# One core, four graph layers in fp32: the second group of tokens shares resident tiles of w0, and two preparations get later keys

## The chip, the cores and the metric

The kernel runs on one core of one Trainium2 chip. The metric is the device time of one execution in microseconds (us). Three executions of the kernel before took 2164.63, 2165.2 and 2167.5 us; the median is 2165.2 us.

## What is computed

128 graphs of 64 nodes with 512 features pass through four layers; each layer adds its result to x and normalizes. Cut to what matters:

```python
# layer 0: w0 is the weight that this case is about
y = x @ w;  s = y @ a
A = exp(leaky(8 * tanh((s_i + s_j) / 8))) * adj
x = layernorm(x + (A / rowsum(A) * rowsum(adj)) @ x @ w)
# layer 1
weight = adj * exp((x @ Wq.T) @ (x @ Wk.T).T)
x = layernorm(x + weight / rowsum(weight) @ (x @ Wv.T))
# layer 2
q, k = split(X @ Wqk);  v = X @ Wv
w = mask * (q . (adj @ (k * mask))) / sqrt(512)
x = layernorm(x + softmax_over_nodes(w)[:, :, None] * v)
# layer 3: two hypergraph convolutions, 512 -> 1024 -> 512, relu and layernorm between
x = layernorm(x + conv(layernorm(relu(conv(x, W1))), W2))
```

## The kernel before, in words

The 8192 tokens are cut into 32 groups (`NG`) of 256 tokens, two tiles of 128 (`GT = 2`). `run(g)` (L1004) writes down all the work of one group as operations with an engine, a cost, what they read and write, and a key. `prepare_chunk(c)` (L699) prepares the adjacency matrices of two groups at a time: chunk 0 serves groups 0 and 1, chunk 1 groups 2 and 3.

Nothing is issued while this is written down. When everything is known, `Order.run` (L140) goes through the operations as a list scheduler: on each engine, whenever it is free in the planner's own time, the ready operation with the lowest key is taken. So each engine's instruction stream is fixed before the kernel runs, and on the chip each engine goes through its stream in order. Keys come from three places:

- For work outside the groups the key is the value of `order.key` at that point in the code: 0.0 for the first use of v1 (L561), 3.0 for m2 (L625), `BASE[GC * c] - 3.0` for the chunk c > 0 (L700), which is 1.0 for chunk 1, as `BASE[2]` is 4.
- For the work of a group, `keys_by_what_follows` (L105) sets it from how long a chain still follows in the group: the operations of group g start at `BASE[g]` (0, 2, 4, 6, 8, 12, ... for g = 0, 1, 2, ...) and spread over 16.
- Evictions of PSUM get `NOW` (100) subtracted, so that they go first. Loads of streamed weights have their user's key less 1.5.

VectorE operations that read only SBUF and all operations of GpSimd are kept from overlapping by the plan (`port`). TensorE has operations in two forms, on the whole 128 x 128 array and on its quarters or columns, and `choose` (L122) keeps to one form for a stretch. A load is planned only while its key is no more than `AHEAD` = 3.5 above the lowest step not yet started.

A product of a 256 x 512 left side with a 512 x 512 weight is done in seven block products in place of eight (`seven_products`, L848). It needs seven pieces of the weight: three of its four quarters (b11, b21, b22) and four combinations t1 to t4 of quarters, which `combine` (L490) makes with three VectorE subtractions and one of GpSimd. The left side needs four sums of its own (`side_sums`, L828; s[2] is made last, and the last of the seven products needs it).

The pieces come to the products in two ways. `prepare_first` (L544) loads the weight into the ring, makes the pieces there, and both stores them in DRAM and returns the resident pieces; group 0 uses these for w0 and v1 (`first_use`). All other groups call `streamed` (L665), which loads the stored pieces from DRAM into new ring tiles: for w0 four loads, three of 512 KB and one of 256 KB. The ring has 8 tiles of 512 KB. The resident w0 takes four (two raw, two of combinations), the resident v1 the other four. A ring tile comes free when its last planned reader is done.

`gram` (L566) multiplies two weight matrices. m2 is made from the two halves of Wqk: each half is loaded in two parts, so its matmuls come in a first half (four operations, one for each of four PSUM banks) and a second half (four more, into the same banks). Its results are copied by ScalarE, and `combine` makes its pieces. m2 is first used by group 0's layer 2.

What happens for a group in its first steps, in order: a dot product per row and two small matmuls with exponentials in between give the attention `e`; `e` is multiplied with the reciprocal of its row sums (L1036); `gathered` (L806) multiplies it on quarters of TensorE with x, ScalarE copies the two banks (gT); `left_side` makes the four sums; seven products with w0 are added to x by VectorE (`scaled_into`, L904), where the last product u goes into two blocks; `layer_norm` (two statistics, a power of -0.5 on GpSimd at L940, a VectorE product, two ScalarE passes); then the transposes (L788), the products with m1 and v1, and so on.

`prepare_chunk` makes four small VectorE operations (L706 to L709), one of GpSimd into `bh` (L711), 32 quarter matmuls (L725), their evictions, five tiny VectorE operations, and, at a key 6.0 higher, two loads of mask rows and two products for `am`, which is first read in layer 2 of the chunk's first group.

In the profile all engine instructions carry line 1178, that of the recording helper, so tile names tell them apart: `ring` is a weight piece, `k` a left side or a raw weight, `e` the attention, `m` the pieces of m1 and m2, `kept` and `bh` belong to the chunk, `w` and `v` are the stored pieces of w0 and v1 in DRAM (`v` those of v2 too).

Of the kernel before, what the change touches and what calls it, by code (L numbers as in the profile page):

```python
# [22 lines left out]
GC = CT // GT  # L23
# [5 lines left out]
BASE = [APART * g - 2 * min(g, 4) - 2 * max(g - NG + 3, 0) for g in range(NG)]  # L29
# [230 lines left out]
def kernel(  # L260
# [51 lines left out]
    order = Order({k: len(v) for k, v in kinds.items()})  # L312
# [309 lines left out]
    for h in range(2):  # L622
        load_half(wq2_raw, wqk_h[0], h)
        load_half(wk2_raw, wqk_h[1], h)
    order.key = 3.0  # L625
    m2 = gram("m2", wq2_raw, wk2_raw, KC // 2)

    order.key = 6.0
# [36 lines left out]
    def streamed(which, room=()):  # L665

        pieces = []
        chunks = KH // 2 if which == "3b" else KC // 2
        for src, n in stored[which]:
            width = PIECE // src.cells  # L670
            t_ = Buf("ring")
            order.add("SP", 500, [src[list(range(n))]], [t_, *(room if not pieces else ())],
                      lambda t_=t_, src=src, n=n, width=width: nc.sync.dma_start(
                          out=t_.t[:, : n * width], in_=src.t[:, : n * width]),
                      urgent=1.5, size=P * n * width * 4)
            for k in range(n):
                pieces.append((t_, lambda t_=t_, k=k, width=width: t_.t[:, ts(k, width)].rearrange(
                    "p (c o) -> p c o", c=chunks)))
        return pieces
# [17 lines left out]
        dma(P * T * 4, [rows], [mask_rows], lambda: mask_rows.t.rearrange("(t p) -> t p", p=P), lambda: flat(rows.t)[:T])  # L697

    def prepare_chunk(c):  # L699
        order.key = BASE[GC * c] - 3.0 if c else 0.5  # L700
        adj, turned = adjs[c], turned_adjs[c]
        m = mask_c.t[:, ts(c, CT)]
        hA, bh, am = Buf("kept"), Buf("bh", 2), Buf("kept")
        be = Buf("col")

        dve(W, [turned], [hA, turn], lambda: nc.vector.tensor_scalar(hA.t, turned.t, 0.0, None, ALU.not_equal))  # L706
        dve(W, [hA], [be], lambda: nc.vector.tensor_reduce(be.t[:, :CT], hA.t, AX.X, ALU.add))
        dve(CT, [be], [be], lambda: nc.vector.tensor_scalar(be.t[:, :CT], be.t[:, :CT], 1.0, None, ALU.max))
        dve(CT, [be], [be], lambda: nc.vector.reciprocal(be.t[:, :CT], be.t[:, :CT]))  # L709

        pool(W, [hA, be], [bh[0]], lambda: nc.gpsimd.tensor_mul(bh.t[:, :, :N], hA.t, per_tile(be.t[:, :CT])))  # L711
        act(CT, [turned], [bh[1]], lambda: nc.scalar.copy(bh.t[:, :, N : N + 1], turned.t[:, :, 0:1]))


        ps = [Buf("bank") for _ in range(2)]
        gm, sums = Buf("kept"), Buf("col")

        def quarters_of(n, at, left, right):
            for g in range(CT // 2):
                for h, (cols, _) in enumerate(halves):  # L720
                    for t, (rows, _) in enumerate(halves):
                        nc.tensor.matmul(ps[t].t[cols, at(g) : at(g) + n], left.t[rows, 2 * g + h], right(2 * g + h)[rows],
                                         start=True, stop=True)

        def emit_g():  # L725
            quarters_of(N + 2, lambda g: (N + 3) * g, hA, lambda i: bh.t[:, i])
            quarters_of(1, lambda g: (N + 3) * g + N + 2, turned, lambda i: ones)

        pe(400, [turned, hA, bh], [*ps, gm], emit_g, mode="quarters", matmuls=16)
        def per_g(t):  # L730
            return ps[t].t[:, : CT // 2 * (N + 3)].rearrange("p (g k) -> p g k", k=N + 3)

        for t in range(2):
            act(P, [ps[t]], [gm], lambda t=t: nc.scalar.copy(
                gm.t.rearrange("p (g t) i -> p t g i", t=2)[:, t], per_g(t)[:, :, :N]), NOW)
            dve(6, [ps[t]], [sums], lambda t=t: nc.vector.tensor_copy(
                sums.t[:, : 3 * CT].rearrange("p (k g t) -> p t g k", t=2, k=3)[:, t],
                per_g(t)[:, :, N:]), NOW)
        dn, n_edges, radj = (slice(CT * k, CT * (k + 1)) for k in range(3))
        g1, dc, dh = Buf("col"), Buf("col"), Buf("col")  # L740

        dve(CT, [sums], [dc], lambda: nc.vector.tensor_scalar(dc.t[:, :CT], sums.t[:, dn], TINY, None, ALU.max))
        dve(CT, [dc], [dc], lambda: nc.vector.reciprocal(dc.t[:, :CT], dc.t[:, :CT]))
        dve(CT, [sums, dc], [dc], lambda: nc.vector.scalar_tensor_tensor(
            dc.t[:, :CT], sums.t[:, dn], 0.0, dc.t[:, :CT], ALU.is_gt, ALU.mult))
        dve(CT, [dc], [dh], lambda: nc.vector.tensor_scalar(dh.t[:, :CT], dc.t[:, :CT], 0.5, None, ALU.mult))

        dve(CT, [dc, sums], [g1], lambda: nc.vector.tensor_mul(g1.t[:, :CT], dc.t[:, :CT], sums.t[:, n_edges]))

        order.key += 6.0  # L750
        mr = Buf("adj", 2)
        for h, (rows, _) in enumerate(halves):
            src = mask_rows.t.rearrange("(t h i) -> h t i", h=2, i=N)[h, ts(c, CT)]
            dma(P * CT * N * 2, [mask_rows], [mr[h]], lambda rows=rows: mr.t[rows],
                lambda src=src: bass.AP(tensor=src.tensor, offset=src.offset, ap=[[0, N], *src.ap]))
        pool(W, [adj, mask_c, turn], [am], lambda: nc.gpsimd.tensor_mul(am.t, adj.t, per_tile(m)))
        dve(W, [am, mr], [am], lambda: nc.vector.tensor_mul(am.t, am.t, mr.t))
        prepared[c] = adj, turned, gm, am, sums, g1, dc, dh
# [89 lines left out]
    def seven_products(a, s, pieces, first, more, across=False):  # L848


        going, pair = Buf("product"), [Buf("bank") for _ in range(2)]
        pieces = iter(pieces)

        def times(ps, left, start=True):
            piece, view = next(pieces)
            token = pair[ps] if isinstance(ps, int) else ps
            chunks = KH // 2 if left[2] else KC // 2
            width = PIECE // chunks if left[2] or wide else D // 2

            def emit():  # L860
                l, b, o = left[1](), view(), token.t
                if across:
                    for c in range(2):
                        for k in range(chunks):
                            nc.tensor.matmul(o[:, ts(c, P)], b[:, k, ts(c, P)], l[:, k, :],
                                             start=start and k == 0 and c == 0,
                                             stop=k == chunks - 1, skip_group_check=True)
                else:
                    for k in range(chunks):
                        nc.tensor.matmul(o[:, :width], l[:, k, :], b[:, k, :], start=start and k == 0,  # L870
                                         stop=k == chunks - 1, skip_group_check=True)

            pe(w_pe(P, 2 * chunks) if across else w_pe(width, chunks), [left[0], piece, going], [token], emit,
               matmuls=2 * chunks if across else chunks)
            return (token, going), lambda: token.t[:, :width]

        deep = a["deep"] if "deep" in a else False
        wide = a["wide"] if "wide" in a else False

        def side(v):  # L880
            return v[0], v[1], deep


        first("11", *times(0, side(a["11"])))
        first("22", *times(1, side(s[0])))
        more("11", *times(Buf("bank"), side(a["12"])))
        first("12", *times(0, side(s[1]), False))
        more("12", *times(1, side(s[3]), False))
        first("21", *times(Buf("bank"), side(a["22"])))
        u = times(0, side(s[2]), False)  # L890
        more("22", *u)
        more("21", *u)
# [11 lines left out]
    def scaled_into(at, f, own, n, base=None):  # L904


        def add(k, token, ps, base):
            dst = at[k]
            t = own.start + int(k[0]) - 1
            dve(n + 40, [*token, f, base[0]], [dst[0]], lambda: nc.vector.scalar_tensor_tensor(  # L910
                dst[1](), ps(), f.t[:, t : t + 1], base[1](), ALU.mult, ALU.add), NOW)

        return (lambda k, token, ps: add(k, token, ps, base[k] if base else at[k]),
                lambda k, token, ps: add(k, token, ps, at[k]))
# [89 lines left out]
    def run(g):  # L1004
# [20 lines left out]
        for t in range(GT):  # L1025
# [12 lines left out]
        step(1)  # L1038
        left = left_side(gathered(*of_x, lambda h, t: e.t[halves[h][0], t, :], [e]))
        step(2)  # L1040
        seven_products(*left, first_use["w0"] if g == 0 else streamed("w0"), *scaled_into(
            at_x, sums, slice(2 * CT + own.start, 2 * CT + own.stop), D // 2))
        layer_norm(xt)

# [204 lines left out]
```

## Time and profile before

| what | value |
|---|---|
| median of three executions | 2165.2 us |
| the profiled execution's own time | 2166.22 us |
| its span, first to last instruction | 2164.4 us |
| VectorE busy | 1541.9 us, 71% of the span |
| ScalarE busy | 856.9 us |
| GpSimd busy | 386.1 us |
| moved by DMA | 476.34 MB, 220 GB/s in the mean |
| granted TensorE clock, mean | 0.998 |

The profiled execution lies 1.82 us above its own span and 1.02 us above the median. After the first groups, which start closer together, results are stored at alternating distances of 65.6 and 66.0 us, one group each: 528.3, 593.8, 659.8, 725.4 us and so on up to about 1700 us. The last four groups end closer together again. A reader should look at the first 65 us by themselves: there groups 0 and 1 start, the weights arrive, and m1 and m2 are made.

### The profile page before, as it was taken

The page shows a single profiled execution, that of the slowest core. Times are in us where ns is not written, and L with a number is a line of the kernel's source. Part 1 is how long each engine was busy: PE and PEld are TensorE (multiplying, and loading weights), DVE is VectorE, ACT ScalarE, POOL GpSimd, SP SyncE. Part 2 cuts the span into 40 slices and gives each one's busy share as a digit, 9 for nine tenths or more (in the row PEclk, how much of TensorE's full clock was granted, in tenths as well). Part 3 has the DMA queues.
Part 4 walks back from the last instruction along what each step waited for, and adds up shares of the span by engine and source line. Part 5 has one row for each costly group of instructions (what it writes and reads, how often), then busy time and mean ns, then how long its engine had stood idle before and what let it go on. Part 6 is the DMA issues. An engine that isn't in the chain of part 4 may idle for free.

```text
span 2164.4 us, 51412 instructions
## 1 busy us (share of the span) xinstructions
PE 2142.8 (99%) x20831; PEld 1717.2 (79%) x20831; DVE 1541.9 (71%) x3967; ACT 856.9 (40%) x1812; POOL 386.1 (18%) x399
## 2 busy tenths in 40 slices
PE   7999999999999999999999999999999999999998
PEld 4887777887888787887878887878877888878866
DVE  6777767677776776776777776777766777766675
ACT  2444343343433433443433434434334333343433
POOL 1113121021201212101222111212012211012120
PEclk9999999999999999999999999999999999999999
DMA  8866668666666667665666665666666666655475
GB/s 276 309 217 224 210 203 282 224 218 235 223 210 205 207 218 240 212 218 198 204 234 220 226 200 207 212 235 224 212 203 210 221 232 213 212 189 207 160 256 198
DMA packets 174364, 476.34 MB, mean 220 GB/s; under 512 B 35824, under 2 KB 45360, under 8 KB 174128
## 3 DMA queue, kind: packets, MB, share of 16 engines
q1 hardware_dynamic: 174128, 473.05, 64.4%
q8 instruction: 165, 2.70, 0.5%
q14 instruction: 71, 0.58, 0.1%
HBM read 443.33 MB, written 29.66 MB: 219 GB/s over the span
## 4 chain that ended last, share of the span: by engine, by line
PE 97%; DMA 2%; DVE 0%; ACT 0%; SPq 0%; issue 0%; POOL 0%; POOLq 0%; DVEq 0%; ACTq 0%
PE bank L1178 97%; DMA x<-in_x_dram 0%; DMA k<-in_wk_dram 0%; DMA ring<-in_wv_dram 0%; DMA k<-in_wqk_dram 0%; DMA v<-ring 0%; DMA ring<-w 0%; SPq L1178 0%; ACT k L1178 0%; DVE k L1178 0%; ACT x L1178 0%; DVE x L1178 0%; DVE col L1178 0%; POOL ring L1178 0%; POOLq L1178 0%
## 5 line engine op out<-in xcount | busy, mean ns | idle before, releaser
L1178 PE MATMUL bank<-ring,k 128*128 128x256 f32 (+1 forms) x3968 | 1035.4, 410 | 7.0 <-DMA ring<-w 4.9
L1178 PEld LDWEIGHTS bank<-ring,k 128*128 128x128 f32 x3968 | 730.3, 190 | 211.3 <-issue 111.2
L1178 ACT COPY k<-bank 128x512 f32<-128x512 f32 (+1 forms) x640 | 304.6, 501 | 603.3 <-PE bank L1178 405.7
L1178 DVE SCALAR_TENSOR_TENSOR x<-bank,col,x 128x256 f32<-128x256 f32 (+1 forms) x832 | 400.7, 500 | 198.8 <-PE bank L1178 187.4
L1178 PEld LDWEIGHTS bank<-k,m 128*128 128x128 f32 x3584 | 427.2, 192 | 22.2 <-issue 13.5
L1178 PE MATMUL bank<-k,m 128*128 128x128 f32 x3584 | 437.0, 276 | 0.0
L1178 PE MATMUL bank<-ring,h 128*128 128x256 f32 (+1 forms) x1408 | 412.0, 439 | 0.0
L1178 POOL TENSOR_TENSOR col<-col,mhalf 128x2 f32<-128x2 f32 (+1 forms) x161 | 111.4, 692 | 1476.8 <-DVE col L1178 634.0
L1178 PEld LDWEIGHTS bank<-ring,h 128*128 128x128 f32 x1408 | 260.1, 190 | 90.0 <-issue 64.3
L1178 ACT ACTIVATE x<-x,col,col 128x512 f32<-128x512 f32 x256 | 197.3, 809 | 168.7 <-DVE col L1178 168.5
L1178 DVE TENSOR_TENSOR k<-bank,k 128x256 f32<-128x256 f32 x384 | 154.0, 421 | 129.1 <-PE bank L1178 123.2
L1178 DVE BATCH_NORM_STATS2 col<-x 128x6 f32<-128x512 f32 x256 | 175.3, 688 | 4.5
L1178 DVE SCALAR_TENSOR_TENSOR h<-bank,col,b3a_b 128x512 f32<-128x512 f32 x128 | 95.9, 750 | 70.5 <-PE bank L1178 69.9
L1178 ACT ACTIVATE k<-bank,u_c 128x128 f32<-128x128 f32 x256 | 80.0, 364 | 133.2 <-PE bank L1178 131.7
L1178 ACT ACTIVATE h<-h 128x512 f32<-128x512 f32 x128 | 80.6, 631 | 127.5 <-DVE h L1178 127.4
L1178 ACT ACTIVATE h<-h,col,col 128x512 f32<-128x512 f32 x128 | 96.8, 807 | 73.6 <-DVE col L1178 73.6
L1178 DVE TENSOR_TENSOR k<-k 128x256 f32<-128x256 f32 x226 | 95.8, 425 | 41.0 <-ACT k L1178 40.6
L1178 PEld LDWEIGHTS bank<-k,k 128*64 128x64 f32 (+1 forms) x2112 | 77.3, 140 | 51.4 <-DVE k L1178 24.2
L1178 PE MATMUL bank<-k,k 128*64 128x64 f32 (+1 forms) x2112 | 105.7, 237 | 6.7 <-DMA k<-in_wk_dram 4.8
L1178 DVE SCALAR_TENSOR_TENSOR h<-bank,col,h 128x512 f32<-128x512 f32 x128 | 93.3, 748 | 22.7 <-PE bank L1178 20.6
L1178 POOL TENSOR_TENSOR x<-x,bv_b 128x512 f32<-128x512 f32 x64 | 81.1, 1271 | 92.0 <-PE bank L1178 68.4
L1178 POOL TENSOR_TENSOR k<-k,b3b_b 128x512 f32<-128x512 f32 x64 | 81.3, 1270 | 79.1 <-DVE k L1178 31.4
(96 smaller groups left out, 1494.4 us busy)
## 6 DMA issues: line engine op xcount, KB each, us to landing
ring<-3a SPq DMA_DIRECT2D x224, 512.0 KB, 4.6
ring<-3b SPq DMA_DIRECT2D x224, 512.0 KB, 4.4
ring<-v SPq DMA_DIRECT2D x189, 512.0 KB, 3.8
ring<-w SPq DMA_DIRECT2D x93, 512.0 KB, 3.3
x<-in_x_dram SPq DMA_DIRECT2D x32, 512.0 KB, 4.6
ring<-v SPq DMA_DIRECT2D x63, 256.0 KB, 4.0
out_dram<-x SPq DMA_DIRECT2D x31, 512.0 KB, 3.0
ring<-w SPq DMA_DIRECT2D x31, 256.0 KB, 4.1
```

The costliest lines, as they stand in the source:

```text
L1178: made = f(*args, **kwargs)
```

## The change

Three places are edited. Group 1, too, takes the resident pieces of w0 (its four loads of stored pieces fall away, and w0's four ring tiles are held until group 1's last product with w0). The key of m2's matmuls, copies and combinations goes from 3.0 to 5.0. The key of chunk 1's preparation goes from 1.0 to 2.5 (the part at `order.key += 6.0` from 7.0 to 8.5); later chunks keep theirs.

```diff
@@ -622,7 +622,7 @@
-    order.key = 3.0
+    order.key = 5.0
     m2 = gram("m2", wq2_raw, wk2_raw, KC // 2)
@@ -697,7 +697,7 @@
     def prepare_chunk(c):
-        order.key = BASE[GC * c] - 3.0 if c else 0.5
+        order.key = BASE[GC * c] - (3.0 if c > 1 else 1.5) if c else 0.5
@@ -1038,7 +1038,7 @@
-        seven_products(*left, first_use["w0"] if g == 0 else streamed("w0"), *scaled_into(
+        seven_products(*left, first_use["w0"] if g < 2 else streamed("w0"), *scaled_into(
             at_x, sums, slice(2 * CT + own.start, 2 * CT + own.stop), D // 2))
```

## The prediction

> **What bounds the kernel now.** I read the page first, for how much there is to win at all, then the waits of TensorE, then the timeline of the stretch in which the longest of them lies, and last a table by windows for the clock.
>
> ```profile
> span 2164.4 us, 51412 instructions
> ...
> PE 2142.8 (99%) x20831; PEld 1717.2 (79%) x20831; DVE 1541.9 (71%) x3967; ACT 856.9 (40%) x1812; POOL 386.1 (18%) x399
> ...
> PE   7999999999999999999999999999999999999998
> ```
>
> TensorE is idle for 2164.4 - 2142.8 = 21.6 us, and the slices put it into the first and the last. Everything between is set by TensorE's own work: the other engines have room and a change of order there can win nothing but a few turns between array forms. The waits of TensorE over the whole span:
>
> ```profile
> PE bank L1178 <- DMA ring<-w: 4.9, 1, 4.9
> PE bank L1178 <- DMA k<-in_wk_dram: 4.8, 2, 4.1
> PE bank L1178 <- DMA k<-in_wqk_dram: 1.8, 1, 1.8
> PE bank L1178 <- ACT k L1178: 1.7, 3, 1.2
> PE bank L1178 <- POOL bh L1178: 0.5, 1, 0.5
> PE bank L1178 <- DVE k L1178: 0.5, 1, 0.5
> ```
>
> The longest is a single wait for stored pieces of w0. The two for in_wk and in_wqk are the first loads of the kernel, and the ScalarE waits lie at the end; the change touches neither. The timeline of TensorE around the wait (start, duration, then the idle time before it in brackets):
>
> ```profile
> 39.91 7.03 PE L1178 MATMUL bank<-k,k 128*128 128x512 f32 x16
> 47.47 0.46 PE L1178 MATMUL bank<-bh,kept 64*64 64x66 f32 x16 [0.53 <-POOL bh L1178]
> ...
> 47.95 1.14 PE L1178 MATMUL bank<-e,x 64*64 64x64 f32 x64
> 49.02 1.13 PE L1178 MATMUL bank<-ring,k 128*128 128x256 f32 x4
> 55.02 2.04 PE L1178 MATMUL bank<-ring,k 128*128 128x256 f32 x4 [4.86 <-DMA ring<-w]
> ...
> 57.97 2.71 PE L1178 MATMUL bank<-ring,k 128*128 128x256 f32 x8 [0.48 <-DVE k L1178]
> ```
>
> In order: m2's second half, chunk 1's quarter matmuls, group 1's gather, group 0's last product with w0 (u), and then group 1's first product, 4.86 us late. Why so late is in SyncE's timeline: the loads are issued when u has freed the ring, and the first lands 4.67 us after its issue (the chain of waits shows 50.21 to 54.88).
>
> ```profile
> 50.21 0.54 SPq L1178 DMA_DIRECT2D ring<-w  x1
> ...
> 51.74 1.94 SPq L1178 DMA_DIRECT2D ring<-w  x3
> ```
>
> VectorE decides when the neighbours of the stall can run:
>
> ```profile
> 42.32 2.37 DVE L1178 TENSOR_TENSOR ring<-ring,ring 128x512 f32<-128x512 f32 x2 [0.41 <-DMA ring<-in_wv_dram]
> 44.61 0.28 DVE L1178 TENSOR_SCALAR kept<-adj 128x256 f32<-128x256 f32 x1
> ...
> 45.68 0.26 DVE L1178 TENSOR_TENSOR e<-e,e 128x128 f32<-128x128 f32 x1
> 45.85 0.42 DVE L1178 TENSOR_TENSOR k<-k 128x256 f32<-128x256 f32 x1
> ```
>
> After v1's combinations come chunk 1's four operations (44.61 to 45.76), then the last factor of group 1's e, then group 0's s[2], which u needs. And the clock, by windows (the third from the end is the granted clock):
>
> ```profile
> 50.00:55.00 5.00, 0.15 (x1) 0.01 (x1) 4.03 (x12) 0.75 (x3) 1.17 (x2) 0.76 0.82 249
> 55.00:60.00 5.00, 4.50 (x12) 3.54 (x13) 2.08 (x7) 2.21 (x5) 0.16 (x1) 0.55 0.93 351
> ```
>
> **What the Trainium skill says.** "TensorE: Matmul & The Clock Gate", Part 1, says that the array falls to half its clock after an idle window of about 3.4 us and needs as long a busy stretch to come back. The trace agrees: after 4.86 us of idle the clock is 0.55 in 55 to 60 us, and four 128x256 matmuls take 2.04 us where the same form takes 1.13 us at 49.02. "DMA: Bandwidth & Descriptors", anatomy of one DMA, gives a fixed part of about 2.0 us and a part by size; the 4.67 us seen here is longer than that sum for 512 KB (an estimate of 3.2 us), in a stretch where the DMA share in the windows is 0.82 to 0.93. "SBUF — State Buffer", two separate sides, says that VectorE operations with two SBUF inputs and GpSimd exclude each other. Here the two v1 subtractions take 2.37 us beside a GpSimd one, where two of m2 take 1.41 us alone.
>
> **The change, part by part.**
>
> *Group 1's w0 is resident.* Four DMAs leave SyncE's queue, 1.75 MB; at the 300 GB/s of 50 to 60 us that is 6 us of transfer. The 4.86 us go as a wait for DMA. So does the slow clock after it: 2.04 - 1.13 for the first product, 0.63 against 0.38 for the two e,same matmuls behind it (the same pair at 64.90), 2.71 - 1.89 for the next eight (the same form at 61.40): 0.91 + 0.25 + 0.82 = 2.0 us. What is late next is group 1's left side: the gather must run, ScalarE copies two banks (1.07 us in the row at 49.13), VectorE makes the sums. On before's schedule gT was there at 50.20, so the part alone would leave no wait longer than the 0.05 us from u's end at 50.15.
>
> *Chunk 1 at 2.5.* I worked the group keys out from `keys_by_what_follows`: group 1's last factor of e has 1.94, group 0's s[2] 2.18, u 2.27, group 1's gather 3.01, its products 3.42 to 4.27. So e and s[2] pass chunk 1's four VectorE operations, which took 1.07 us: they end near 44.9 and 45.3 instead of 45.9 and 46.3. v1's combinations, key 0.0, stay ahead. On TensorE the 32 quarter matmuls (0.8 us) lose their place in front of the gather and come when `bh` is ready, between products; the 0.53 us wait for it goes, as there is other work. Its first user is group 2's first w0 eviction, of step 5.75. The two mask loads, the GpSimd product and the VectorE product for `am` move from 7.0 to 8.5; their reader has a key near 11.8. I cost them at nothing: they lie beside TensorE's work of 60 us and more, and if the cover went, a load of 64 KB (8.8 us to landing) would be the price.
>
> *m2 at 5.0.* Its matmuls do not vanish and stay the filler: at 39.9 us nothing else is ready in this trace, as e and s[2] wait for VectorE until 44.9. So about three of the four second-half operations (1.75 us each, 7.03 / 4) still run there. The gather (3.01 against 5.0) and u then pass the rest, which is left for the 1.1 us in which ScalarE copies gT. If the plan thinks e is ready sooner than it is, the stream has two before the gather, and TensorE idles from 43.4 to 44.9: 1.5 us, which I take as the bad end, with 0 as the good one. The 4 copies of m2's banks hold up to four of eight PSUM banks longer; a shortage makes m2 the only thing that can run and so ends itself. The VectorE operations at 52.34 (1.41 us) stood between the statistics of group 0 (ending 52.43) and its power on GpSimd at 54.44, a wait of 3.8 us put down to VectorE; at key 5.0 they leave that place. m2 is read by group 0 at key 6.54 and after, some 40 us on.
>
> *The new stretch.* From 44.9: gather 1.1, u 0.95, the rest of m2 1.75, chunk 1's 0.8, seven products at about 0.9 = 6.3: 10.9 us, to about 55.8. Group 0's normalization starts with u's evictions at about 47.2; before, it took from 49.02 to transposes at 60.52, of which 3.8 us were the wait for the port and 2.7 us (55.16 to 57.83) VectorE standing behind the stalled eviction. Without these it is about 5 us after u's end, so transposes at 52 to 54 and m1's first product at about 55. It meets the end of the stretch, with perhaps 1 us to spare or to miss. I put new gaps (side sums, copies, this meeting) at 1.7 us, between 0.5 and 4.
>
> *Sum.* 4.86 + 2.0 + 0.53 + 0.48 = 7.87 removed, 1.7 added: 6.2 us. The profiled execution's 2166.22 becomes 2160.0; the median lies 1.02 us below that execution, so 2159.0. All later work moves up as a block, since TensorE has only two gaps, of 0.08 and 0.14 us, between 200 and 1900 us; the tail (3 waits of 1.7 us, then about 7 us after the last matmul) I leave as it is, give or take 1.5 us.
>
> **Rivals.**
>
> *The stall is only halved.* The plan orders e or the gather too early or too late for the chip, group 1's left side comes at 50 us as before, and TensorE idles near 3 us, with half of the slow clock. For it: VectorE is 70 to 90% busy here and works in order. Against: e passes 1.07 us of work. Of 7.87, 3 + 1 are kept as loss: 3.9 us won, 2161.3, inside 0.2%.
>
> *The ring is the next wait.* w0 holds four tiles until group 1's last product, v1 the other four until group 0's. No stream can start before about 50 us; group 2's w0 and group 1's v1 follow each other there. If SyncE meets a tile not yet free, a v1 piece arrives a load (4.9 us) late, and with the slow clock 6.9 us are back: 2165.9. Against: before, the same tiles were taken by group 1's stream until 58 to 68 us, and nothing stalled between 60 and 160.
>
> *Slower: the order locks into another cycle.* The plan of all 32 groups follows from the first 65 us. Before, it settles into pairs of 131.6 us, about 13 of them. Between neighbouring starts in the trace, going from the whole array to quarters takes 309 ns where whole to whole takes 216, and going back 148: about 0.22 us for an excursion, some ten in a pair. Four more in each pair are 0.9 us, x 13 = 11.7 us, less the 6.2 won: 2170.7. It decides from 0.48 us a pair. Against: keys and costs of groups 4 and later are unchanged, and the stores' alternation from the fifth group on says that the start is forgotten soon.
>
> **How the numbers follow.** The forecast 0.66, the halved stall 0.16, the ring 0.06, the other cycle 0.12. A measurement here can tell about 0.2%, 4.3 us, from no change. Faster: 0.66. Within: 0.16 + 0.06 = 0.22. Slower: 0.12. The range runs from 2156.5 (0.5 us of new gaps and a tail better by 1.3) to 2166.0, which takes in the halved stall and the ring; the other cycle and the forecast's lowest part, about 0.2, are left out. The forecast's own range is 2156.5 to 2161.
>
> **What would show it.** Right: no wait for ring<-w, granted clock near 1.0 in 50 to 60 us, the e factor ahead of chunk 1's operations on VectorE, group 0's transposes at 52 to 54 us, stores 6 us earlier from the first to the last. Wrong: TensorE waits over 1.5 us before 60 us on VectorE or ScalarE (the halved stall), a wait on ring<-v (the ring), or stores whose distance is not 131.6 us a pair (the cycle).

## The result, and the profile after

The changed kernel takes 2160.19 us (median of 10 executions, 2159.08 to 2160.87), the kernel before 2165.15 us (10 executions). The ratio is 0.9975, with a 95% interval of 0.9967 to 0.9983: 5.0 us or 0.25% faster, where 6.2 us were forecast. The two profiled executions took 2166.22 and 2160.18 us, 6.0 us apart.

First the page of the changed kernel, its span and TensorE's line, then all of TensorE's waits:

```profile
span 2158.4 us, 51427 instructions
...
PE 2141.8 (99%) x20825; PEld 1716.0 (80%) x20825; DVE 1541.6 (71%) x3967; ACT 856.1 (40%) x1812; POOL 385.4 (18%) x399
```

```profile
PE bank L1178 <- DMA k<-in_wk_dram: 4.6, 2, 4.2
PE bank L1178 <- DVE k L1178: 2.0, 2, 1.3
PE bank L1178 <- ACT k L1178: 1.7, 3, 1.2
PE bank L1178 <- ACT m L1178: 0.7, 1, 0.7
```

The span is 6.0 us shorter, and idle time accounts for most of it: 21.6 us before, 2158.4 - 2141.8 = 16.6 now. The 4.9 us for ring<-w are gone, with the 0.5 for bh; the waits on VectorE have grown from 0.5 to 2.0 in two pieces. Of the wait of 1.8 us for in_wqk, one of the kernel's first loads, only 0.7 (on ScalarE's m) is left; that lies at 24 us, ahead of anything that the change moves on TensorE. The remaining 1.0 us is less busy time. From group 0's first product with w0 to the end TensorE is busy for 1.9 us less (2115.03 us before, 2113.13 now), as matmuls that ran slowly no longer do; ahead of it for 0.8 us more. The stretch itself, in TensorE's timeline of the changed kernel:

```profile
39.37 5.31 PE L1178 MATMUL bank<-k,k 128*128 128x512 f32 x12
44.52 1.03 PE L1178 MATMUL bank<-ring,k 128*128 128x256 f32 x4
45.48 1.16 PE L1178 MATMUL bank<-e,x 64*64 64x64 f32 x64
46.57 1.98 PE L1178 MATMUL bank<-k,k 128*128 128x512 f32 x4
48.48 0.46 PE L1178 MATMUL bank<-bh,kept 64*64 64x66 f32 x16
...
49.05 1.99 PE L1178 MATMUL bank<-ring,k 128*128 128x256 f32 x8
...
53.45 0.66 PE L1178 MATMUL bank<-ident,x 128*128 128x128 f32 x4 [1.32 <-DVE k L1178]
```

Three of m2's four second-half operations run, then u, the gather, m2's last operation, chunk 1, and at 49.05 group 1's first two products, without a gap up to 52. The one left is before group 0's transposes. VectorE's timeline shows why u and the gather are earlier:

```profile
41.41 2.36 DVE L1178 TENSOR_TENSOR ring<-ring,ring 128x512 f32<-128x512 f32 x2
43.69 0.28 DVE L1178 TENSOR_TENSOR e<-e,e 128x128 f32<-128x128 f32 x1
43.89 0.42 DVE L1178 TENSOR_TENSOR k<-k 128x256 f32<-128x256 f32 x1
44.23 0.28 DVE L1178 TENSOR_SCALAR kept<-adj 128x256 f32<-128x256 f32 x1
```

e and s[2] now stand between v1's combinations and chunk 1. And the clock, by windows of the changed kernel (the window and its length, busy time of TensorE, its weight loads, VectorE, ScalarE and GpSimd, then the granted clock, the DMA share and GB/s):

```profile
50.00:55.00 5.00, 3.68 (x21) 2.95 (x20) 3.78 (x14) 3.29 (x9) 0.10 (x1) 1.00 0.94 303
55.00:60.00 5.00, 5.00 (x32) 4.59 (x31) 3.52 (x8) 1.59 (x4) 2.40 (x2) 1.00 1.07 366
```

Stores of group 3 and later come 6.1 to 6.6 us earlier (521.7 in place of 528.3 for group 5, 2154.8 in place of 2161.2 for the last), with about 131.6 us for two groups as before. Those of groups 1 and 2 gain 7.6 and 11.2 us, and group 0's comes later: 283.4 after 282.8.

### The profile page after: what moved, and what is told of

It is laid out like the page before. It is cut to its first block, busy times and chain, and to the rows that moved or that the text cites. A ratio compares the mean times of both kernels' runs of the same rounds, so it can differ in the third digit from the quotient of the medians.

```text
span 2158.4 us, 51427 instructions
## 1 busy us (share of the span) xinstructions
PE 2141.8 (99%) x20825; PEld 1716.0 (80%) x20825; DVE 1541.6 (71%) x3967; ACT 856.1 (40%) x1812; POOL 385.4 (18%) x399
## 4 chain that ended last, share of the span: by engine, by line
PE 98%; DMA 1%; DVE 0%; SPq 0%; ACT 0%; issue 0%; ACTq 0%; DVEq 0%
PE bank L1178 98%; DMA k<-in_wk_dram 0%; SPq L1178 0%; DMA adj<-in_adjT_dram 0%; DMA x<-in_x_dram 0%; DVE k L1178 0%; DVE x L1178 0%; ACT k L1178 0%; ACT x L1178 0%; DVE col L1178 0%; ACT m L1178 0%; ACT e L1178 0%; DVE e L1178 0%; ACT bh L1178 0%; ACTq L1178 0%
```

## The experiments

Each was timed beside the kernel before on the same chip; three chips were used. Because the first loads of the kernel arrive at slightly different times, single profiled executions reach group 0's first product with w0 anywhere from 33.43 to 34.74 us (one at 36.79, below). For a comparison of profiles I therefore also give the *rest*: the span less the start of that product. Before it is 2164.4 - 34.49 = 2129.9 us, for the changed kernel 2158.4 - 33.95 = 2124.5: 5.5 us less before rounding. Waits and clock account for it: TensorE's gaps from 38 to 210 us sum to 5.93 before and 1.95 after, its busy time is the 1.9 us less given above, and the part behind the last matmul is 0.4 us longer (7.5 in place of 7.1).

The rest is still one execution's. Two profiles of the changed kernel agree in it within 0.1 us, but the median of the times lies between 33.8 us (w0_alone) and 38.6 us (keys_urgent) above the rest; if the rest were free of chance, the distance would be the same for all. The profiled executions of w0_alone, keys_alone and chunk_alone were 1.9, 1.5 and 1.0 us above their medians, that of w0_m2 1.6 below. So a difference of 1 to 2 us in the last two columns can be that of an execution.

| kernel | ratio to before (95%) | gaps 38 to 210 us | rest |
|---|---|---|---|
| before | 1 | 5.93 | 2129.9 |
| changed | 0.9975 (0.9967 to 0.9983) | 1.95 | 2124.5 |
| w0_alone | 0.9993 (0.9985 to 1.0001) | 5.71 | 2130.6 |
| chunk_alone | 0.9992 (0.9986 to 0.9999) | 3.88 | 2129.5 |
| keys_alone | 0.9990 (0.9982 to 0.9999) | 4.50 | 2129.2 |
| w0_m2 | 0.9995 (0.9987 to 1.0003) | 3.54 | 2127.8 |
| w0_chunk | 0.9977 (0.9968 to 0.9986) | 2.32 | 2124.5 |
| w0_s2 | 0.9986 (0.9980 to 0.9993) | 3.21 | 2126.2 |
| keys_urgent | 0.9986 (0.9979 to 0.9992) | 1.09 | 2124.8 |
| changed_again | 0.9979 (0.9969 to 0.9988) | 2.19 | 2124.4 |
| bh_after | 0.9973 (0.9963 to 0.9983) | 1.56 | 2123.5 |
| s2_first | 0.9987 (0.9981 to 0.9994) | 4.11 | 2128.6 |
| chunk_31 | 0.9973 (0.9964 to 0.9982) | 2.04 | 2124.8 |
| before_filled | 0.9998 (0.9990 to 1.0006) | 1.86, with 4.3 of filling | 2129.7 |

### The parts one by one

*w0_alone*, the shared tiles with the old keys:

```diff
-        seven_products(*left, first_use["w0"] if g == 0 else streamed("w0"), *scaled_into(
+        seven_products(*left, first_use["w0"] if g < 2 else streamed("w0"), *scaled_into(
```

> Group 1 takes the resident w0; both keys stay at 3.0 and 1.0. Theory A (the reload of w0 is the cost: 4.9 us of wait and 2.0 us of slow clock): the wait for ring<-w is gone, group 1's first product starts at about 50.2 us, right behind u, the granted clock is 1.0 in 50 to 60 us, and 1.5 to 3 us come back as waits on VectorE, because m2's combinations still stand before group 0's power: 2160.5 to 2162 us. Theory B (the keys do the work, the residence alone only changes what is waited for): group 1's left side is no earlier, TensorE idles over 4 us elsewhere before 60 us: 2164 to 2165.5 us.

It measured 2164.39 us beside 2165.94: theory B's range, though the longest wait is shorter than the 4 us that B named. In its TensorE timeline:

```profile
48.74 4.09 PE L1178 MATMUL bank<-ring,k 128*128 128x256 f32 x16
56.01 0.61 PE L1178 MATMUL bank<-e,same 128*128 128x128 f32 x2 [3.18 <-ACT e L1178]
56.42 5.22 PE L1178 MATMUL bank<-ring,k 128*128 128x256 f32 x16
```

The wait for ring<-w is gone, and u and group 1's first three products run through from 48.74. Then TensorE stands before a small matmul of group 2 (e,same), which the plan has put in front of group 1's other four products. What it waits for (a small ScalarE operation) needs the last of these three rows of VectorE, which stand behind each other:

```profile
52.28 1.07 DVE L1178 SCALAR_TENSOR_TENSOR x<-bank,col,x 128x256 f32<-128x256 f32 x2
...
53.56 1.41 DVE L1178 TENSOR_TENSOR m<-m 128x512 f32<-128x512 f32 x2
54.88 0.68 DVE L1178 SCALAR_TENSOR_TENSOR k<-x,u_b 128x512 f32<-128x512 f32 x1
```

Evictions, m2's combinations, then the row product of group 2 that the small matmul needs. The stall is 3.18 us, and the slow clock comes with it (0.66 in 55 to 60 us). So the removed wait covered another one; the interval of the shared tiles alone, up to 1.0001, leaves open whether they gain anything.

*keys_alone*, both keys later, w0 streamed for group 1:

```diff
-    order.key = 3.0
+    order.key = 5.0
     m2 = gram("m2", wq2_raw, wk2_raw, KC // 2)
-        order.key = BASE[GC * c] - 3.0 if c else 0.5
+        order.key = BASE[GC * c] - (3.0 if c > 1 else 1.5) if c else 0.5
```

> Both keys are later (5.0 and 2.5), group 1 loads stored pieces of w0 as before. Theory A (residence is needed): the loads can be issued only when u has freed the ring; if u ends near 50 us as before, the wait of 4.9 us and the slow clock stay: 2164 to 2165.5 us. Theory B (the keys move u from 49.0 to 44.5 us, so the ring is free at 45.5 and the first piece lands at about 50.2, while m2's last operation and chunk 1's matmuls keep TensorE busy until 49.0): the wait for ring<-w is 1 to 1.5 us, the clock stays at 1.0, and nearly the whole gain is there: 2160 to 2162 us.

2163.68 us, 0.9990: between the two theories, neither's numbers. u moves forward, as theory B says (44.95), yet the wait is 2.71 us, not 1 to 1.5, and the clock falls to 0.50. SyncE's timeline of this run shows what theory B left out:

```profile
46.10 1.35 SPq L1178 DMA_DIRECT2D v<-ring  x2
47.50 2.48 SPq L1178 DMA_DIRECT2D adj<-in_adjT_dram  x3
50.08 0.54 SPq L1178 DMA_DIRECT2D ring<-w  x1
```

Here the first load goes into the ring tile that u has read, so it can't go before 46.1. But SyncE issues two stores of v1 and three loads of chunk 2 first, since their keys (0.0, 1.0) are below the load's 1.92.

*chunk_alone*, only the second of these two keys:

> Chunk 1 at 2.5 alone; m2 at 3.0 and w0 streamed as before. If m2's key does nothing: as the run with both keys alone, 0.999 of before within 0.0004, with a wait for ring<-w of 2 to 3 us. If m2's key was what won 2.3 us there: as before, 2165.5 to 2166.5 us.

0.9992 with a wait of 1.74 us for ring<-w and one of 1.87 for ScalarE's x: as keys_alone within the interval. So nothing that m2's key does can be told here.

*w0_m2* and *w0_chunk*, the shared tiles with one key each:

> Resident w0 and m2 at 5.0, chunk 1 at 1.0 as before. If the place of m2's combinations before group 0's power is what a key is worth: 1 to 2 us less than the run with the resident w0 alone, with e and s[2] still behind chunk 1's four VectorE operations: 2159.5 to 2161 us. If the place of chunk 1 is what counts: no better than the resident w0 alone, within 0.5 us.

> Resident w0 and chunk 1 at 2.5, m2 at 3.0 as before. e and s[2] come at 43.7 to 44.3 us as in the changed kernel, and the gather has to wait behind m2's second half, whose key 3.0 is below 3.01. If chunk 1's place is what a key is worth: as the changed kernel within 1 us, 2160 to 2161 us. If m2's combinations in front of group 0's power matter: 1 to 2 us slower than the changed kernel, with a TensorE wait on VectorE of over 2 us between 50 and 60 us: 2161 to 2162.5 us.

w0_m2 measured 2164.92 us, no better than w0_alone in time; its profiled execution was its fastest and shows gaps of 3.54 us. w0_chunk measured 2160.84 us, 0.9977: the whole gain, without m2's key. Each of its 11 executions was faster than each of the 13 of w0_alone beside it (2162.22 at most, 2162.59 at least). So neither the shared tiles nor chunk 1's key has the gain alone (0.07% and 0.08%, together 0.23%), and m2's later key adds nothing that can be told. Whether the two together give more than their sum the intervals leave open.

### Through what does chunk 1's key work?

*w0_s2* has the shared tiles, leaves both keys as they were and lets group 0's s[2] go first, so that u comes before chunk 1's matmuls and the gather (one line of the edit; `first` is 2.5 for group 0's left side for w0, and 0 elsewhere):

```diff
-        do(s[2], a["11"], a["21"])
+        do(s[2], a["11"], a["21"], urgent=first)
```

> Resident w0 alone, both keys as before, and group 0's side sum s[2] made 2.5 earlier in key, ahead of v1's combinations and of chunk 1's operations on VectorE. Its only effect on TensorE's order is that u comes before chunk 1's matmuls and the gather. Theory (chunk 1's key works through u: group 0's normalization starts earlier, ahead of m2's combinations): u at about 46.3 in place of 48.7 us, the 3.2 us wait on ScalarE's e and the slow clock behind it go or shrink below 1.5 us: 2161 to 2163 us. Rival (what counts is chunk 1's own work leaving VectorE and GpSimd before the gather): as the resident w0 alone, 2163.5 to 2165 us.

```profile
46.64 1.03 PE L1178 MATMUL bank<-ring,k 128*128 128x256 f32 x4
...
50.39 2.86 PE L1178 MATMUL bank<-ring,k 128*128 128x256 f32 x12 [1.16 <-ACT k L1178]
53.87 1.36 PE L1178 MATMUL bank<-ident,x 128*128 128x128 f32 x8 [0.63 <-ACT x L1178]
```

u runs at 46.64 as expected, no gap in this stretch is over 1.16 us, the clock stays at 1.00, and the time is 2163.03 us, at the edge of the theory's range and below the rival's. The ratio is 0.0007 below that of w0_alone, with intervals that overlap, where chunk 1's key brings 0.0016. In the single profiles the rest is 3.7 us below before, out of 5.5 for the changed kernel, and the stall of 3.18 us is gone, with chunk 1 and m2 where they were. So with an earlier u that stall is gone, and it probably carries a part of what chunk 1's key brings; how large a part, and what the remainder is, was not separated.

*s2_first*, the same edit on the changed kernel:

> The changed kernel with the same earlier s[2] for group 0. It comes before v1's combinations, so v1's stores and chunk 1 come 0.4 us later; TensorE's planned order now has the gather before u. Theory (u's time matters, not s[2]'s): no better than the changed kernel, 2160 to 2161 us. If the earlier sum helps by itself: 2158.5 to 2159.5 us.

2163.73 us, 0.9987: slower than both theories have it. TensorE's order changed more than I had foreseen; group 0's transposes wait 1.62 us for ScalarE, and at 126.11 us a product waits 2.29 us for VectorE, where the other kernels' waits from 100 to 140 us are 0.97 at most. In this profile a small edit near 40 us came with a wait of over 2 us at 126.

*keys_urgent* tests the reading of SyncE's queue: keys_alone, with the four loads ahead in key (`streamed` takes by how much; part of one line is shown, before as in keys_alone).

```diff
-first_use["w0"] if g == 0 else streamed("w0")
+first_use["w0"] if g == 0 else streamed("w0", urgent=3.5 if g == 1 else 1.5)
```

> Both keys later, w0 streamed for group 1, but the four loads get a key 2.0 lower, so that SyncE's queue has the first of them ahead of v1's stores and of chunk 2's adj loads, which stood between u's end (46.1 us) and the load's issue (50.1 us) in the run with the keys alone. Theory (with the keys alone it is SyncE's order, not the ring, that keeps the wait): the first piece lands before 50 us, no wait for ring<-w over 0.5 us, clock at 1.0, and the time comes within 1 us of the changed kernel: 2160 to 2161.5 us. Rival (the 1.75 MB of transfer itself crowds out others in 45 to 60 us): another wait for a DMA or for what follows one takes its place, 2162.5 to 2164 us.

```profile
41.88 0.34 SPq L1178 DMA_DIRECT2D ring<-w  x1
...
47.38 0.49 SPq L1178 DMA_DIRECT2D ring<-w  x1
...
49.01 1.56 SPq L1178 DMA_DIRECT2D ring<-w  x2
```

The first load goes out at 41.88, 5.5 us before u begins:

```profile
47.36 1.03 PE L1178 MATMUL bank<-ring,k 128*128 128x256 f32 x4
```

So a load need not wait for u. In the kernel before it wasn't u either, although its load was issued just as u ended. The plan of that kernel puts the first load into the tile that only group 0's first product reads on TensorE (34.49 us), and the second and fourth into tiles that nothing had used. What stands in front of the load at 50.21 is again v1's stores and the loads of adj, issued almost without a break until 50.11:

```profile
46.39 1.47 SPq L1178 DMA_DIRECT2D v<-ring  x2
47.91 2.20 SPq L1178 DMA_DIRECT2D adj<-in_adjT_dram  x3
```

In keys_urgent TensorE's wait for ring<-w is 0.58 us, close to the bound named; all gaps from 38 to 210 us sum to 1.09, less than in the changed kernel, and the rest is 2124.8 us, as there. So the wait can be nearly hidden without shared tiles, by the order of SyncE's queue. The time is not as expected: 2163.36 us over 21 executions from 2160.47 to 2167.43. The profiled execution is the median one. In it the first product with w0 starts 2.6 us later than in keys_alone, with the slow clock from 25 us on, before TensorE's streams differ; without these 2.6 us it would lie in the expected range. Whether the other executions start late too isn't known, so whether this edit gains as much as the changed kernel stays open.

### The slow clock by itself

*before_filled* puts matmuls of constants in front of group 1's first product in the kernel before (`fill` holds one 18, for that product):

```diff
             def emit():
                 l, b, o = left[1](), view(), token.t
+                for _ in range(fill.pop() if fill else 0):
+                    nc.tensor.matmul(o[:, :P], same, ident, start=True, stop=True, skip_group_check=True)
```

> The kernel before, with 18 matmuls of a constant by a constant (two records of 0.11 us each, 4.0 us in all) put in front of group 1's first product with w0, into the bank that this product clears; order and loads as before. They fill the wait for ring<-w without shortening it. Theory (the slow clock after the wait is a cost of its own): the wait shrinks from 4.9 to about 1 us, the granted clock stays at 1.0 in 50 to 60 us, the next matmuls take 1.1 us in place of 2.0, and the time is 1.5 to 2 us below before: 2163.5 to 2164.5 us. Rival (the slow clock costs nothing, because what follows waits for other engines anyway): within 0.5 us of before.

```profile
49.88 4.29 PE L1181 MATMUL bank<-ident,same 128*128 128x128 f32 x36 [0.97 <-DVE x L1181]
54.00 1.03 PE L1181 MATMUL bank<-ring,k 128*128 128x256 f32 x4
54.87 0.38 PE L1181 MATMUL bank<-e,same 128*128 128x128 f32 x2
55.94 1.99 PE L1181 MATMUL bank<-ring,k 128*128 128x256 f32 x8 [0.69 <-DVE k L1181]
...
2143.25 0.68 PE L1181 MATMUL bank<-kept,h 64*64 64x64 f32 x28 [1.69 <-issue]
```

The clock is 1.00, and the rows behind the wait take 1.03, 0.38 and 1.99 us in place of 2.04, 0.63 and 2.71: 2.0 us less, as the prediction had it. The time is 2165.12 us, 0.9998 (0.9990 to 1.0006): nothing that can be told. Part is given back at once (0.69 for VectorE in place of 0.48), and 1.69 us near the end, where a run of 128 small matmuls is broken by a stall that the profile puts down to issue; before, the same run took 2.09 us unbroken. The cost of the clock is shown in the rows, not in the time.

### What is left at 53.45 us

Group 0's transposes wait for ScalarE's normalization passes, these for VectorE's product behind the power. *chunk_31* puts chunk 1 behind that product (0.9 in place of 1.5, a key of 3.1):

> The changed kernel with chunk 1's key at 3.1 in place of 2.5, behind group 0's second normalization product (key 2.98), which in the changed kernel stands on VectorE behind chunk 1's five tiny operations and their waits (power done at 49.7, product at 52.3 us). Theory (this is the 1.3 us wait left at 53.45 us): the product comes at about 50.5, the transposes at 52, and the time is 1 to 1.5 us below the changed kernel: 2158.7 to 2159.3 us where that is at 2160.2. Rival (another wait takes its place, as with the resident w0 alone): the same as the changed kernel within 0.5 us, or slower.

2160.02 us, 0.9973 (0.9964 to 0.9982). The rival holds: other waits take the place, 0.7 us for ScalarE's x and 0.7 for its k. Together with 0.6 for VectorE's k at 161 us, which the changed kernel has too, that makes 2.04 between 38 and 210 us, where the changed kernel has 1.95.

*bh_after* takes another link. ScalarE's copy into bh for chunk 2 stood before group 0's passes; now it waits for VectorE's first operation of its chunk as well, and so comes later in ScalarE's order:

```diff
-        act(CT, [turned], [bh[1]], lambda: nc.scalar.copy(bh.t[:, :, N : N + 1], turned.t[:, :, 0:1]))
+        act(CT, [turned, hA], [bh[1]], lambda: nc.scalar.copy(bh.t[:, :, N : N + 1], turned.t[:, :, 0:1]))
```

> The changed kernel, where ScalarE's small copy into bh (one for each chunk) also waits for VectorE's first operation of its chunk. In the changed kernel the copy for chunk 2 stands on ScalarE before group 2's tanh and group 0's normalization passes, and waits 1.24 us for the load of adj. TensorE's order stays the same over the first 350 rows. Theory (that copy is part of the 1.3 us wait left at 53.45 us): the wait for adj is gone from ScalarE, group 0's passes start at about 51.9 in place of 52.6, TensorE's wait falls to 0.7 us or less, and the time is 0.5 to 1 us below the changed kernel. Rival (the power's product on VectorE, held by evictions, is what is late): TensorE's wait stays at 1.2 to 1.4 us and the time is the same within 0.3 us.

> The changed kernel itself, on the chip of this call, as the measure for the next run. 0.9975 of before, 2160 to 2161 us.

ScalarE in the changed kernel, and then in bh_after:

```profile
51.60 0.20 ACT L1178 COPY bh<-adj 128x4 f32<-128x4 f32 x1 [1.24 <-DMA adj<-in_adjT_dram]
51.71 0.51 ACT L1178 ACTIVATE e<-bank,col 128x64 f32<-128x64 f32 x2
52.58 1.52 ACT L1178 ACTIVATE x<-x,col,col 128x512 f32<-128x512 f32 x2 [0.36 <-DVE col L1178]
```

```profile
51.45 0.52 ACT L1178 ACTIVATE e<-bank,col 128x64 f32<-128x64 f32 x2 [0.95 <-PE bank L1178]
52.33 1.52 ACT L1178 ACTIVATE x<-x,col,col 128x512 f32<-128x512 f32 x2 [0.36 <-DVE col L1178]
```

The wait for adj is gone, and the passes start 0.25 us earlier (0.4 counted from the first product with w0), not the 0.7 expected. TensorE's wait falls to 0.92 us, from 1.32, and from 1.55 in the second profile of the changed kernel: between the theory's 0.7 and the rival's 1.2. bh_after measured 2160.09 us, changed_again 2161.09 on the same chip: 1.0 us, with ratios 0.9973 (0.9963 to 0.9983) and 0.9979 (0.9969 to 0.9988) whose intervals overlap. The profiles show that the copy is a part of the wait; that bh_after beats the changed kernel isn't settled.

## Why the prediction was right, and where not

- *The wait for ring<-w and the slow clock.* Right in place and size: 4.86 and 2.0 us gone; the 2.0 is confirmed row by row in before_filled.
- *"The loads are issued when u has freed the ring."* Wrong as the reason for the late load, and so is the picture of a full ring: in the plan before, v1's combinations take two tiles that w0's products have left, and two tiles stay unused until group 1's loads. SyncE's order held the load (keys_urgent). The forecast didn't suffer, since the shared tiles remove the load whatever held it; but I never priced the simpler edit, an earlier key for four loads.
- *"So the part alone would leave no wait longer than the 0.05 us."* Wrong. The shared tiles alone leave 3.18 us at another place and the slow clock with it. I followed group 1's left side, which was indeed in time, and not the matmul of group 2 that stands between its products in TensorE's order.
- *Chunk 1's key.* The order came out as worked out from the keys (e and s[2] ahead, about 1.1 us nearer to v1's combinations). But I valued it at a 0.53 us wait; on top of the shared tiles it is worth 0.9977 against 0.9993, some 3.5 us, a part of it probably because u and group 0's normalization come before the row products and combinations crowd VectorE (w0_s2).
- *m2's key.* Three of four operations ran before u, as said, and the idle end of 1.5 us did not occur. The power came at 48.97 in place of 54.44 us. Yet w0_chunk has the whole gain without that key, as u had moved by then: cost and benefit nothing that can be told.
- *Group 0's normalization, "about 5 us after u's end".* It took 7.9 (45.5 to 53.45 us): VectorE's product behind the power stood 2.6 us behind evictions, chunk 1's tiny operations and a wait for ScalarE. The transposes fell within the 52 to 54 us forecast only because u was earlier than I had it: it ran ahead of the gather, not behind, and ended at 45.5 us in place of about 47. That was luck.
- *New gaps, 1.7 us.* 1.95 us were measured between 38 and 210 us, but only 1.32 of them where I had put them; 0.64 lies at 161 us, where I expected none. The sum is near by chance.
- *Sum.* 6.2 us forecast; 6.0 between the profiled executions, 5.5 in the rest, 5.0 between the medians. That the two profiles agree so well with the forecast is in part luck, since 0.5 us of their distance is the earlier start of the first product with w0. The 1.2 us between forecast and medians is mostly the anchor: I took the profiled execution 1.02 us above the median as a fixed distance, but the changed kernel's lies at its own median (2160.18 and 2160.19). That part is how one execution falls, not the change.
- *Stores 6 us earlier "from the first to the last".* From group 3 on yes, groups 1 and 2 more than that; group 0's came 0.6 later, perhaps because its work now shares TensorE with group 1's sooner, which was not tested.
- *The rivals.* Neither the ring nor another cycle: there is no wait for ring<-v, and the pairs stay at about 131.6 us. The halved stall is what w0_alone, keys_alone and chunk_alone look like; the three edits together escape it, if closely: the wait before group 0's transposes was 1.32 us in one profile and 1.55 in the other, where I had named 1.5 as the sign of being wrong, and the clock stayed at 1.00 in both.

## What to carry to other kernels

A long wait can cover a second one on another engine: before you price its removal, follow every instruction in the waiting engine's own order behind it, also those of other work, and not only the chain that it served. When a load comes late, look at what its queue issued just before it, even if something else happened to end at the same moment. Order changes that can hardly be told one by one can be worth more in pairs, so test pairs before calling one of them useless. When medians and single profiles differ by a microsecond or two, subtract the part of the profile that the edit can't reach, and remember that what is left is still one execution.

## What the runs showed of the hardware that was not expected

The slow clock can follow a shorter wait than the one studied. In keys_urgent a wait of 1.98 us at 24.77 us, after one of 0.97 at 11.02, was followed by four 128x512 matmuls in 2.84 us, where the kernel before, after a wait of 1.85 at the same place, took 1.95; the granted clock was 0.72 in 24 to 30 us. changed_again had a wait of 1.92 there and kept its clock. The Trainium skill, "TensorE: Matmul & The Clock Gate", Part 1, names an idle window of about 3.4 us that runs freely; a wait of 1.98 us alone does not fill it, and no run here shows what else decides. Two more traces show a fall before 3.4 us of unbroken waiting. In chunk_alone waits of 1.87 us (before 50.90) and 1.74 us (before 54.00), with 1.36 us of matmuls between them, were followed by four 128x256 matmuls in 2.04 us, where the same form takes 1.03 at 63.19. In the kernel before, the long wait began at 50.15 us, and the granted clock was already 0.82 in 52 to 53 us and 0.50 in 53 to 54.

36 more matmul records at 50 us came with a stall of 1.69 us put down to issue in a run of small matmuls 2090 us later, whose operations were the same. Its cause wasn't tried.
